# Accumulating DMA transfers for a quarter of the global attention's running sums, and an add on VectorE for the horizontal units

## The chip, the core and the metric

The kernel runs on one core of a Trainium2 chip. Its engines work side by side, each through its own queue of instructions in order: PE (TensorE, matmuls), DVE (VectorE), ACT (ScalarE), POOL (GpSimd) and SP, which here only issues DMA transfers. They wait for one another by semaphores. The metric is the time of one execution on the device in microseconds; several runs are given by their median.

## What is computed

Two layers on eight images of 64 x 64 pixels and 256 channels, all in float32. The first layer has attention in windows of 8 x 64 pixels (horizontal, half of the channels) and 64 x 8 (vertical, the other half), plus a depthwise 3 x 3 convolution, and an output projection. The second has attention of every pixel with all 4096 pixels of its image.

```
# layer 0, cut
s = einsum('bwhtd,bwhsd->bwhts', q, k) / sqrt(d)      # 512 x 512 a window and head, d = 32, 4 heads
a = softmax(s, axis=-1)
ctx = einsum('bwhts,bwhsd->bwhtd', a, v)              # v is k
context = hard_swish(concat(ctx_h, ctx_v) + conv3x3(hard_swish(k)) + bias)
x = context @ w_out + b_out
# layer 1, cut
s = einsum('bnd,bmd->bnm', g, f)                      # 4096 x 4096 an image, d = 32
beta = softmax(s, axis=-1)
v = einsum('bnm,bmd->bnd', beta, h)
out = gamma * (v @ kv + bv) + x
```

The sums of the softmax are what the change is about. The kernel computes exponentials without subtracting a maximum, multiplies them with the values, and divides by their sum afterwards.

## The kernel before

**Units and steps.** An image is cut into units: eight horizontal (`h`), eight vertical (`v`) and two global ones (`l`). A horizontal unit has four steps, a vertical one three, a global one 32. In each step PE computes the scores of 128 keys against four blocks of 512 queries (for a window unit the blocks are the four heads, for a global unit four blocks of pixels), in two PSUM tiles of 128 x 1024. ACT takes the exponential of each (`weights_of`, line 543) and writes a weight tile `p` of 128 partitions (keys) x 4 rows x 512 columns. PE multiplies that with the values into `num` (`weighted`, lines 811, 804 and 1005). The weight tiles come from a pool of three buffers: the exponential of a step can't begin before all readers of the tile three steps earlier are done.

**Sums.** The sum over the keys is a product with a matrix of ones. To spend little of PE on it, VectorE first adds weight tiles into `acc` (128 x 2048), and PE multiplies only the result. In a global unit VectorE adds all 32 tiles (`add`, lines 1014 and 1016: 31 adds), and `sums` (line 1025) makes four products of 512 columns, one for each row, into the four quarters of PE's columns. In a horizontal unit VectorE adds only the tiles of steps 0 and 1 (line 820); `sums` (line 842) then makes three terms: the tile of step 2, that of step 3 in two halves of 256 columns, and `acc` in two halves. ACT copies the sums out of PSUM (line 563), VectorE turns them into reciprocals and multiplies (`norm`). `acc` has one buffer for all units, so a unit's first add waits until the sums before it have been read by PE.

**Order.** The order of all instructions is made by a planner when the kernel is built (`Flow`). Scores and values of the steps form its spine. All else (projections of the next image's input, convolution taps, sums, normalisations, transfers) are tasks in lanes (`pe`, `dve`, `act`, `sp`, `pool` and more) with a due step, needs, and estimated costs (the constants ADD, PROD and so on). Between two steps it fills PE, ACT and VectorE by due time as its own clocks allow. `readers` makes it place the adds that read a weight tile before the exponential that overwrites it. The engines then follow that fixed order. The units run in the order h1 to h7, v0 to v7, h0 of the next image, l0, l1, so that projections and convolution of the next image fill the global stage.

**POOL** writes the zero borders of the convolution's input `hv` (memsets, lines 670 to 675) and copies the rows that two tiles share (lines 678 and 679), and relays a bank from one matmul to another in vertical units. It issues no DMA. The transfers that the kernel has are issued by SP, and at the start by ACT.

`raw` holds the weights of the second layer's three projections until they have been combined with the output projection; `h_sb` holds the turned values `h` of the global attention (written at line 954).

Of the kernel before, what the change touches and what calls it, by code (L numbers as in the profile page):

```python
# [23 lines left out]
D = 32  # L24
NQ = P // D
# [5 lines left out]
def quad(r):  # L31
    return slice(r * D, (r + 1) * D)
# [8 lines left out]
def side(h):  # L41
# [5 lines left out]
DUE = dict(  # L47
    near_k=-4, near_q=0, near_values=-14, clip=-12, swish=-1,
    conv_h0=24, conv_h1=10, conv_h2=10, conv_h3=14, conv_v0=1, conv_v1=8, conv_v2=10, conv_v3=8,
    tap=-10, join_h=13, join_hl=20, join_v=9, context=0, norm=1, release=-8, sums=8, add=-6, adds_h=0, adds_v=0, group_h=0, group_v=1, add2=3, apart=4,  # L50
    fg0=-7, fg2=-2, fg3=20, h0=1, h1=10, values_v=-12, near0=-4, spread0=13, spread1=61,
    conv_first=3, far_swish=1,
)
# [5 lines left out]

SCORES, VALUES, PROD, TURN, DRAIN, PASS, THIRD = 0.96, 0.88, 0.86, 0.65, 0.11, 0.43, 0.5  # L60
EXP, EVICT, COPY, VIEW = 0.97, 0.62, 0.52, 0.42
ADD, NORM, SWISH, TAP, TAPS = 2.36, 2.5, 0.75, 0.75, 1.28
PE_LAG, LAG, SLACK = 0.28, 0.1, 0.3
ISSUE, LOAD, VIA, FETCH, HALO, BEHIND = 0.6, 4.3, 2.6, 2.8, 0.6, 3.0

# [20 lines left out]
class Flow:  # L86
# [5 lines left out]
    def __init__(self):  # L92
        self.t = 0
        self.clock = dict(pe=0.0, act=0.0, dve=0.0, sp=0.0)
        self.lanes = dict(pe=[], turn=[], act=[], dve=[], sp=[], pool=[], res=[])
        self.open = None
        self.held, self.held_more, self.values_due = None, 0.0, False
        self.bank_free = 0.0
        self.half_end = self.exp_end = 0.0
        self.third = False  # L100
        self.apart = 0
# [122 lines left out]
    def step(self, scores, values, passes=2, third=False):  # L224

        c = self.clock
        more = (passes - 2) * PASS
        rest = None  # L230
        self.third = passes > 2
        self.apart += 1
        self.values_due = True
        for task in self.waiting("res"):
            if self.apart >= DUE["apart"] and task.begin() <= c["pe"] + DRAIN or not scores:
                self.apart = 0
                c["pe"] = max(c["pe"] + DRAIN, self.half_end + LAG)
                while not task.done:
                    self.fill_act(c["pe"] + 4 * PROD)
                    self.run(task)  # L240
                    self.fill_dve()
        if scores:
            rest = scores()
            c["pe"] = max(c["pe"], self.banks()) + DRAIN + SCORES + more
            self.third = third
            self.half_end = max(c["act"], c["pe"] - more + PE_LAG) + EXP
            if more:
                self.half_end = max(self.half_end, c["pe"] + PE_LAG) + EXP
            before, self.exp_end = self.exp_end, self.half_end + EXP
            c["act"] = self.exp_end  # L250
        else:
            before = self.exp_end
            c["pe"] = self.half_end = self.exp_end = max(c["pe"], c["act"], c["dve"]) + 3.0
        for task in sorted(self.waiting("turn"), key=lambda k: k.due):
            if self.begin(task) <= c["pe"] + 0.1:
                self.run(task)
        urgent = sorted((k for k in self.lanes["pe"] if k.due <= self.t), key=lambda k: k.due)
        if len(urgent) > 1 and urgent[0] in self.waiting("pe"):
            if self.begin(urgent[0]) <= c["pe"] + 0.1:
                self.require(urgent[0])  # L260
        if self.held:
            self.held()
            c["pe"] = max(c["pe"] + DRAIN, before + LAG) + VALUES + self.held_more
        self.held, self.held_more, self.values_due = values, more, False
        if rest:
            rest()
        self.fill_act(self.late(c["pe"]) - EVICT)
        self.fill_pe()
        self.fill_act(self.late(c["pe"]) + SLACK)
        self.fill_dve()  # L270
        for task in self.waiting("sp"):
            if task.begin() <= self.clock["pe"] + 0.5:
                self.run(task)

        for task in self.waiting("pool"):
            if task.begin() + BEHIND <= self.clock["pe"]:
                self.run(task)
        self.t += 1
# [19 lines left out]
def tile_attention_blocks(  # L298
# [18 lines left out]
    nc = tc.nc  # L317
# [26 lines left out]
    nc.sync.dma_start(out=wqkv_sb, in_=w_qkv.rearrange("(k p) m -> p k m", p=P))  # L344
    bqkv_sb = const.tile([P, 4], F32, name="bqkv_sb")
    nc.sync.dma_start(out=bqkv_sb, in_=b_qkv)
    raw = const.tile([P, 2, 3, D], F32, name="raw")
    for z in range(3):
        nc.scalar.dma_start(out=raw[:, :, z, :], in_=wfgh[z].rearrange("(k p) m -> p k m", p=P))

# [34 lines left out]


    NF = 3 * D + 3
    flat = raw.rearrange("p k z d -> p k (z d)")
    ext = prep.tile([P, 2, NF], F32, name="ext")
    a_f = prep.tile([P, 2, 3], F32, name="a_f")  # L390
    nc.vector.tensor_mul(
# [69 lines left out]
    def attention(images, load_x, out_rows, exact):  # L461
# [9 lines left out]
            tc.tile_pool(name=f"dram{sfx}", bufs=2, space=bass.MemoryType.DRAM)  # L471
        )
        ptp = pools.enter_context(tc.tile_pool(name=f"ptp{sfx}", bufs=3))
        ps_sc = pools.enter_context(tc.tile_pool(name=f"ps_sc{sfx}", bufs=1, space=PSUM))
        ps_av = pools.enter_context(tc.tile_pool(name=f"ps_av{sfx}", bufs=1, space=PSUM))

# [2 lines left out]
        act = [state.tile([P, 2, 2 * TB], F32, name=f"act{i}") for i in range(NB // 2)]  # L479
        f4 = state.tile([P, N], F32, name="f4")  # L480
        gq = state.tile([P, 2, TB], F32, name="gq")
        h_sb = state.tile([P, N // P, D], F32, name="h_sb")


        pairs = deque(ps_sc.tile([P, 2, TB], F32, name=f"s_{i}") for i in range(3))
# [99 lines left out]
        def image(b):  # L585
# [374 lines left out]
            def global_unit(z):  # L960
                nm = f"{b}_l{z}"
                u = {}
# [38 lines left out]
                def weighted(c):  # L1001
                    if c == 0:
                        u["num"] = ps_av.tile([P, TB], F32, tag="num", name=f"num_{nm}")
                    for r in range(NQ):
# [2 lines left out]
                            start=(c == 0), stop=(c == 4 * NB - 1),  # L1007
                        )

                def add(c):  # L1010

                    if c == 1:
                        u["acc"] = work.tile([P, NQ, TB], F32, tag="acc", name=f"acc_{nm}", bufs=1)
                        nc.vector.tensor_add(u["acc"], u[0], u[1])
                    else:
                        nc.vector.tensor_add(u["acc"], u["acc"], u[c])  # L1016
# [5 lines left out]
                def sums():  # L1022
                    u["sum"] = mm_tile(f"sum_{nm}")
                    for r in range(NQ):
                        nc.tensor.matmul(  # L1025
                            u["sum"][quad(r), :], lhsT=ones[:, :D], rhs=u["acc"][:, r, :],
                            start=True, stop=True,
                        )
                    copy_sums(u, nm)

                def norm():
# [40 lines left out]
                def last_ends(m, js):  # L1072
# [12 lines left out]
                        nc.sync.dma_start(out=out_rows(b, m)[:, i * TB : (i + 1) * TB], in_=ot)  # L1085

                return SimpleNamespace(
                    steps=4 * NB, scores=scores, weighted=weighted, add=add,
                    release=release, sums=sums, norm=norm, result=result,
                    last_blocks=last_blocks, last_ends=last_ends,  # L1090
                )
# [57 lines left out]
        for u in units:  # L1149
# [4 lines left out]
            if u.kind == "l":  # L1154
                chain = None
                for c in range(1, u.steps):
                    task = flow.add(
                        "dve", [(partial(u.add, c), [("dve", ADD)])], u.t + c + DUE["add"],
                        [w[c]] + ([w[0]] if c == 1 else [chain]), ready=u.t + c + 1,
                    )  # L1160
                    if c == 1:
                        in_turn("acc", task)
                        readers[u.t].append(task)
                    readers[u.t + c].append(task)
                    chain = task
                total = flow.add(
                    "pe", [(u.sums, [("pe", PROD), ("act", COPY)])], e + 1, [chain], ready=e, bank=True
                )
                in_turn("sum", total)
                last_users["acc"].append(total)  # L1170
# [360 lines left out]
```

## Time and profile before

| | |
|---|---|
| runs | 3416.8, 3414.51, 3416.49 us; median 3416.49 |
| profiled execution, span from first to last instruction | 3412.2 us |
| mean granted TensorE clock | 0.996 |
| adds of global units (line 1016), 128x2048 | 480 of 2.291 us, 1099.7 us in all |
| first adds of global units (line 1014) | 16 of 2.292 us |
| adds of horizontal units (line 820) | 64 of 2.283 us |
| exponentials of global units (line 543), 128x1024 | 1024 of 1.025 us, in 512 pairs |
| one convolution tap on VectorE (line 691) | 1.280 us, 512 of them |
| bytes moved by DMA | 210 MB, mean 62 GB/s |

The span is that of one profiled execution; the runs' times are a little longer, since they hold what lies around the instructions. Busy shares say how much of the span an engine executed something; a matmul's end is modelled, and a PE that waits for a short time can look busy. The columns of the windows view, for each stretch of time, are its length, then busy time and number of instructions of PE, of its weight loads (PEld), DVE, ACT and POOL, then the granted clock, the DMA engines' busy share, and GB/s.

### The profile page before, as it was taken

How to read it: one execution, taken by the hardware profiler on the slowest of the kernel's cores; microseconds unless marked ns; L12 is line 12 of the kernel's file. 1: busy time of each engine (PE TensorE's matmuls, PEld its weight loads, DVE VectorE, ACT ScalarE, POOL GpSimd, SP SyncE). 2: the span in 40 equal slices, each digit the busy share in tenths (PEclk: the TensorE clock that was granted, in tenths of full speed). 3: DMA queues.
4: the chain of work that ended last, by engine and by line, in shares of the span. 5: the costliest groups of instructions: out<-in, count | busy, mean ns of one | idle time of the engine just before them, and what ended most of it. 6: DMA issues, size and time to landing. Idle time of an engine off the chain costs nothing. (4 is left out here: it accounts for less than half of the span.)

```text
span 3412.2 us, 83293 instructions
## 1 busy us (share of the span) xinstructions
PE 3353.6 (98%) x36340; PEld 1260.9 (37%) x36340; DVE 2799.7 (82%) x2340; ACT 2663.0 (78%) x3235; POOL 55.4 (2%) x264
## 2 busy tenths in 40 slices
PE   7999999999999999999999999999999999999998
PEld 3343333533335333353334433344333443334422
DVE  4789798986989779897798887988879888798886
ACT  5778787887778877788778887788877888778776
POOL 0000000000000000000000000000000000000000
PEclk9999999999999999999999999999999999999999
DMA  2132103221033111231112311123111231122201
GB/s 71 51 91 67 50 14 103 85 57 57 19 95 93 49 54 38 88 89 49 44 44 86 93 42 51 51 82 92 42 43 57 86 88 40 38 62 71 73 21 39
DMA packets 249428, 210.13 MB, mean 62 GB/s; under 512 B 26080, under 2 KB 190432, under 8 KB 249056
## 3 DMA queue, kind: packets, MB, share of 16 engines
q1 hardware_dynamic: 246816, 204.18, 20.1%
q8 instruction: 287, 4.70, 0.6%
q10 hardware_dynamic: 2240, 0.56, 0.1%
q14 instruction: 85, 0.70, 0.1%
HBM read 99.78 MB, written 83.89 MB: 54 GB/s over the span
## 5 line engine op out<-in xcount | busy, mean ns | idle before, releaser
L1016 DVE TENSOR_TENSOR acc_l<-acc_l,p_l 128x2048 f32<-128x2048 f32 x480 | 1099.7, 2291 | 229.9 <-ACT p_l L543 204.0
L543 ACT ACTIVATE p_l<-s 128x1024 f32<-128x1024 f32 x1024 | 993.3, 1025 | 202.9 <-PE s L989 136.1
L691 DVE SCALAR_TENSOR_TENSOR act<-hv,dw_sb,act 128x1024 f32<-128x1024 f32 x512 | 654.9, 1280 | 29.5 <-ACT act L687 15.9
L989 PE MATMUL s<-gq,f 32*128 32x512 f32 x4096 | 631.6, 639 | 1.6 <-ACT p_l L543 1.0
L543 ACT ACTIVATE p_h<-s 128x1024 f32<-128x1024 f32 x512 | 494.2, 1023 | 76.7 <-PE s L782 49.3
L1005 PE MATMUL num_l<-p_l,h_sb 128*32 128x512 f32 x4096 | 545.5, 605 | 2.1 <-ACT nums_l L1020 2.1
L294 PE MATMUL pq<-x,wqkv_sb 128*32 128x256 f32 x8192 | 533.2, 383 | 3.0 <-ACT qh L617 1.6
L294 PEld LDWEIGHTS pq<-x,wqkv_sb 128*32 128x32 f32 x8192 | 264.3, 111 | 380.2 <-issue 237.4
L782 PE MATMUL s<-qh,kh 32*128 32x512 f32 x2048 | 316.2, 640 | 9.7 <-ACT qh L617 5.7
L989 PEld LDWEIGHTS s<-gq,f 32*128 32x128 f32 x4096 | 195.0, 182 | 300.4 <-issue 282.7
L811 PE MATMUL num_h<-p_h,vs 128*32 128x512 f32 x2048 | 272.8, 605 | 5.3 <-DMA vs<-kvia 3.5
L759 PE MATMUL s<-qv,kv 32*128 32x256 f32 x3072 | 242.1, 402 | 8.3 <-ACT p_v_m L776 8.3
L294 PE MATMUL s<-act,wout_sb 128*32 128x512 f32 x2048 | 226.7, 594 | 0.1
L1005 PEld LDWEIGHTS num_l<-p_l,h_sb 128*32 128x32 f32 x4096 | 80.6, 108 | 386.1 <-issue 371.3
L804 PE MATMUL num_v<-p_v,vs 128*32 128x256 f32 x2048 | 197.5, 382 | 0.0
L1054 ACT ACTIVATE ot_l<-s,bias_o 128x512 f32<-128x512 f32 x120 | 76.0, 684 | 153.0 <-PE s L294 140.4
L759 PEld LDWEIGHTS s<-qv,kv 32*128 32x128 f32 x3072 | 145.9, 184 | 124.9 <-ACT p_v L771 34.4
L820 DVE TENSOR_TENSOR acc_h<-p_h,p_h 128x2048 f32<-128x2048 f32 x64 | 146.1, 2283 | 18.4 <-PE sum_l L1025 13.2
L771 ACT ACTIVATE p_v<-s 128x1024 f32<-128x1024 f32 x128 | 131.5, 1028 | 35.0 <-PE s L759 35.0
L782 PEld LDWEIGHTS s<-qh,kh 32*128 32x128 f32 x2048 | 92.2, 183 | 174.7 <-issue 136.8
L776 ACT ACTIVATE p_v_m<-s 128x1024 f32<-128x1024 f32 x128 | 131.7, 1029 | 23.1 <-DVE acc_v L827 23.1
L820 DVE TENSOR_TENSOR acc_v<-p_v,p_v 128x2048 f32<-128x2048 f32 x64 | 146.6, 2290 | 0.0
(139 smaller groups left out, 3213.3 us busy)
## 6 DMA issues: line engine op xcount, KB each, us to landing
x<-in_xT SPq DMA_DIRECT2D x92, 512.0 KB, 3.9
kvia<-kt SPq DMA_DIRECT2D x128, 256.0 KB, 2.3
vs<-kvia SPq DMA_DIRECT2D x512, 64.0 KB, 2.0
out<-ot_l SPq DMA_DIRECT2D x128, 256.0 KB, 2.1
via_v<-nums_v SPq DMA_DIRECT2D x64, 256.0 KB, 2.0
shuf_v<-via_v SPq DMA_DIRECT2D x256, 64.0 KB, 2.0
f<-fg SPq DMA_DIRECT2D x256, 64.0 KB, 2.0
gq<-fg SPq DMA_DIRECT2D x64, 64.0 KB, 2.0
```

The costliest lines, as they stand in the source:

```text
L294: nc.tensor.matmul(out[quad(r), :], lhsT=lhsT[:, quad(r)], rhs=rhs, start=start, stop=stop)
L543: nc.scalar.activation(pt[:, 2 * z : 2 * z + 2, :], sc[z], AF.Exp, scale=scale)
L691: nc.vector.scalar_tensor_tensor(o, src, wt, o, ALU.mult, ALU.add)
L759: mm = nc.tensor.matmul(place_of(n, r, h, sc), lhsT=k[quad(r), t * P : (t + 1) * P], rhs=q[quad(r), side(h)], start=True, stop=True,)
L776: nc.scalar.activation(pm, mid, AF.Exp, scale=D**-0.5)
L782: nc.tensor.matmul(row_of(sc, r), lhsT=k[quad(r), c * P : (c + 1) * P], rhs=q[quad(r), :], start=True, stop=not exact,)
L804: nc.tensor.matmul(u["num"][quad(r), side(h)], lhsT=vs[kind, i][:, r, t, :], rhs=place_of(n, r, h, (pt[:, :2], u["mid", c], pt[:, 2:])), s ...
L811: nc.tensor.matmul(u["num"][quad(r), :], lhsT=vs[kind, i][:, r, c, :], rhs=u[c][:, r, :], start=(c == 0), stop=(c == 3),)
L820: nc.vector.tensor_add(u["acc"], u["acc"] if c == 2 else u[0], u[c])
L989: nc.tensor.matmul(row_of(sc, r), lhsT=f4[quad(r), c * P : (c + 1) * P], rhs=gq[quad(r), z, :], start=True, stop=not exact,)
L1005: nc.tensor.matmul(u["num"][quad(r), :], lhsT=h_sb[:, c, :], rhs=u[c][:, r, :], start=(c == 0), stop=(c == 4 * NB - 1),)
L1016: nc.vector.tensor_add(u["acc"], u["acc"], u[c])
```

## The change

Three parts.

1. Global units: VectorE adds only rows 0 to 2 of each weight tile (1536 columns in place of 2048). Row 3 (128x512, 256 KB) is summed by DMA transfers that POOL issues: steps 0 and 1 are copied, the even steps to row 3 of `acc` and the odd steps to a tile `row` of its own, and each later step's transfer adds to what lies there. So there are 32 transfers a unit in two chains, 512 in all. The sums' product for row 3 has two parts, `acc` and `row`, one after the other into the same quarter of PE's columns.
2. Horizontal units: `adds_h=1`, so VectorE adds the third weight tile (step 2) into `acc` as well, with a second add of 128x2048; the sums then have the tile of step 3 as one product of 512 columns, and `acc` in two halves.
3. To have room for `row`, `h_sb` becomes a constant tile, and `raw` a view of its first six blocks.

The planner gets a lane `rows` for the transfers, with estimated costs of 1.0 and 3.0, and a smaller cost for the add.

```diff
-    tap=-10, ... adds_h=0, adds_v=0, ...
+    tap=-10, ... adds_h=1, adds_v=0, ...
...
-ADD, NORM, SWISH, TAP, TAPS = 2.36, 2.5, 0.75, 0.75, 1.28
+ADD, ADD3, NORM, SWISH, TAP, TAPS = 2.36, 1.83, 2.5, 0.75, 0.75, 1.28
+GATHER, SUMMED = 1.0, 3.0
...
+        for task in self.waiting("rows"):
+            if task.begin() <= self.clock["pe"] + 0.5:
+                self.run(task)
         for task in self.waiting("pool"):
...
-    raw = const.tile([P, 2, 3, D], F32, name="raw")
+    h_sb = const.tile([P, N // P, D], F32, name="h_sb")
+    raw = h_sb[:, : 2 * 3, :].rearrange("p (k z) d -> p k z d", k=2)
...
+        rowp = None if exact else pools.enter_context(tc.tile_pool(name="rowp", bufs=1))
...
-        h_sb = state.tile([P, N // P, D], F32, name="h_sb")
...
+                rows = NQ if exact else NQ - 1
+
+                def acc_tile():
+                    if "acc" not in u:
+                        u["acc"] = work.tile([P, NQ, TB], F32, tag="acc", name=f"acc_{nm}", bufs=1)
+                    return u["acc"]
+
                 def add(c):
 
-                    if c == 1:
-                        u["acc"] = work.tile([P, NQ, TB], F32, tag="acc", name=f"acc_{nm}", bufs=1)
-                        nc.vector.tensor_add(u["acc"], u[0], u[1])
+                    acc = acc_tile()[:, :rows, :]
+                    nc.vector.tensor_add(acc, u[0][:, :rows, :] if c == 1 else acc, u[c][:, :rows, :])
+
+                def gather(c):
+
+                    if c < 2:
+                        u["row", c] = (
+                            rowp.tile([P, TB], F32, tag="row", name=f"row_{nm}")
+                            if c else acc_tile()[:, rows, :]
+                        )
+                        nc.gpsimd.dma_start(out=u["row", c], in_=u[c][:, rows, :])
                     else:
-                        nc.vector.tensor_add(u["acc"], u["acc"], u[c])
+                        nc.gpsimd.dma_start(out=u["row", c % 2], in_=u[c][:, rows, :], accum_op=ALU.add)
...
                     for r in range(NQ):
-                        nc.tensor.matmul(
-                            u["sum"][quad(r), :], lhsT=ones[:, :D], rhs=u["acc"][:, r, :],
-                            start=True, stop=True,
-                        )
+                        parts = [u["acc"][:, r, :]] if r < rows else [u["row", 0], u["row", 1]]
+                        for k, part in enumerate(parts):
+                            nc.tensor.matmul(
+                                u["sum"][quad(r), :], lhsT=ones[:, :D], rhs=part,
+                                start=(k == 0), stop=(k == len(parts) - 1),
+                            )
...
-                        "dve", [(partial(u.add, c), [("dve", ADD)])], u.t + c + DUE["add"],
+                        "dve", [(partial(u.add, c), [("dve", ADD if exact else ADD3)])], u.t + c + DUE["add"],
...
+                gathered = []
+                for c in range(0 if exact else u.steps):
+                    task = flow.add(
+                        "rows", [(partial(u.gather, c), [("pool", GATHER), ("dma", SUMMED)])], u.t + c,
+                        [w[c], *gathered[-2:-1]], gathered[-1:], ready=u.t + c + 1,
+                    )
+                    if c < 2:
+                        task.after += last_users["acc"][-1:]
+                    readers[u.t + c].append(task)
+                    gathered.append(task)
                 total = flow.add(
-                    "pe", [(u.sums, [("pe", PROD), ("act", COPY)])], e + 1, [chain], ready=e, bank=True
+                    "pe", [(u.sums, [("pe", PROD * (1 if exact else 1.5)), ("act", COPY)])], e + 1,
+                    [chain, *gathered[-2:]], ready=e, bank=True,
                 )
```

(`exact` marks a second version of the kernel that runs only where sums leave the range of float32; it does not run here.)

More of the change, by code (lines that the diff above doesn't have):

```diff
@@ L49 @@
     conv_h0=24, conv_h1=10, conv_h2=10, conv_h3=14, conv_v0=1, conv_v1=8, conv_v2=10, conv_v3=8,
-    tap=-10, join_h=13, join_hl=20, join_v=9, context=0, norm=1, release=-8, sums=8, add=-6, adds_h=0, adds_v=0, group_h=0, group_v=1, add2=3, apart=4,
+    tap=-10, join_h=13, join_hl=20, join_v=9, context=0, norm=1, release=-8, sums=8, add=-6, adds_h=1, adds_v=0, group_h=0, group_v=1, add2=3, apart=4,
     fg0=-7, fg2=-2, fg3=20, h0=1, h1=10, values_v=-12, near0=-4, spread0=13, spread1=61,
@@ L94, in __init__ @@
         self.clock = dict(pe=0.0, act=0.0, dve=0.0, sp=0.0)
-        self.lanes = dict(pe=[], turn=[], act=[], dve=[], sp=[], pool=[], res=[])
+        self.lanes = dict(pe=[], turn=[], act=[], dve=[], sp=[], pool=[], rows=[], res=[])
         self.open = None
@@ L387, in tile_attention_blocks @@
     NF = 3 * D + 3
-    flat = raw.rearrange("p k z d -> p k (z d)")
+    flat = h_sb[:, : 2 * 3, :].rearrange("p (k z) d -> p k (z d)", k=2)
     ext = prep.tile([P, 2, NF], F32, name="ext")
@@ L1087, in global_unit @@
                 return SimpleNamespace(
-                    steps=4 * NB, scores=scores, weighted=weighted, add=add,
+                    steps=4 * NB, scores=scores, weighted=weighted, add=add, gather=gather,
                     release=release, sums=sums, norm=norm, result=result,
```

## The prediction

> **What bounds the kernel now.** I read the busy shares first, then one image cut into its stages, then who waits for whom, then single steps.
>
> ```profile
> PE 3353.6 (98%) x36340; PEld 1260.9 (37%) x36340; DVE 2799.7 (82%) x2340; ACT 2663.0 (78%) x3235; POOL 55.4 (2%) x264
> ```
>
> The windows view of one image, with its rows in the order horizontal units 1 to 7, vertical units, unit 0 of the next image, the two global units:
>
> ```profile
> 910.00:1023.40 113.40, 112.67 (x1196) 38.84 (x1192) 96.57 (x101) 86.32 (x109) 5.05 (x16) 1.00 0.27 80
> 1023.40:1118.50 95.10, 94.09 (x1273) 48.97 (x1266) 86.96 (x92) 77.96 (x95) 0.78 (x8) 1.00 0.31 93
> 1118.50:1131.70 13.20, 13.20 (x148) 5.08 (x148) 6.38 (x8) 11.11 (x14) 0.00 (x0) 1.00 0.23 66
> 1131.70:1327.60 195.90, 195.63 (x1930) 63.11 (x1932) 158.74 (x89) 156.79 (x189) 1.11 (x8) 1.00 0.13 39
> ```
>
> PE (second number) fills every stage; VectorE (fourth) has 17 us free in the horizontal stage, 8 in the vertical, 37 in the global one. But PE's ends are modelled, so short waits hide in its busy time. The waits view and two stretches of global steps show them:
>
> ```profile
> ACT p_l L543 <- DVE acc_l L1016: 61.7, 106, 2.2
> ```
> ```profile
> 1308.06 1.94 ACT L543 ACTIVATE p_l<-s 128x1024 f32<-128x1024 f32 x2 [0.46 <-DVE acc_l L1016]
> 1310.46 1.94 ACT L543 ACTIVATE p_l<-s 128x1024 f32<-128x1024 f32 x2 [0.46 <-DVE acc_l L1016]
> ```
> ```profile
> 3271.28 1.94 ACT L543 ACTIVATE p_l<-s 128x1024 f32<-128x1024 f32 x2 [0.25 <-PE s L989]
> 3273.43 1.94 ACT L543 ACTIVATE p_l<-s 128x1024 f32<-128x1024 f32 x2 [0.21 <-PE s L989]
> ```
>
> A step without other matmuls takes 2.40 us where the exponential waits for the add that frees its weight buffer (2.29 plus 0.1), and 2.15 us where it waits for PE. So PE bounds the kernel, except in about 106 global steps, where VectorE's add does.
>
> **Third weights of horizontal units: off PE, onto VectorE.**
>
> ```profile
> 942.77 1.07 PE L811 MATMUL num_h<-p_h,vs 128*32 128x512 f32 x8
> 943.65 1.91 PE L842 MATMUL sum_h<-p_h,ones 128*32 128x512 f32 x24
> 945.37 1.05 PE L842 MATMUL sum_h<-acc_h,ones 128*32 128x256 f32 x16
> ```
>
> From 943.65 to 945.37 run 24 matmuls on the weights: 8 of 512 columns (step 2's weights) and 16 of 256 (step 3's, in two halves). Afterwards step 2's are in the accumulated tile and step 3's make one product of 512. 1.72 us for twice the same work is 0.86 each, so PE loses 64 units x 0.86 = 55.0 us. VectorE gains 64 adds of 128x2048 at 2.29 (146.6 us). A global add shrinks to 1536 columns: the adds of 512 columns (L859, 0.692) and 2048 (2.291) give 1.041 ns a column, so 1.758; 496 x 0.533 = 264 us less. VectorE in all: -118 us. Where this lands is read from the instruction order: between the first add of unit 1 and the first vertical add VectorE gets 7 adds (+16.0) and loses 8 convolution taps (8 x 1.28), 4 swishes, 3 joins or contexts and a transpose (8 x 0.69) and one normalisation (2.4), together -18.2. The global stage takes 11 more taps. So the horizontal stage holds 96.6 - 2.2 = 94.4 us of VectorE work in 113.4 - 7 x 0.86 = 107.4: 88% in place of 85%. What hides the new adds is that room; but the sums' last term now follows 0.86 us after the first and waits in PE's queue for the second add, with the next scores behind it. The nearest row is 20.0 us in 15 waits of p_h for acc_h (1.3 each): doubled, +20; at best 0. I take +8, the convolution work having moved away.
>
> **Fifth sum product of a global unit.** The fourth row's sum is made from two parts into one quarter of PE's columns. Four side by side take 0.97 (below, 1227.23 to 1228.20); one more behind the fourth costs up to 0.86, at least 0 if the next matmuls fill the other quarters. I take 0.86: 16 x 0.86 = +13.8.
>
> **The accumulating transfers.** 512 transfers of 128x512 (256 KB), issued on POOL's queue, two chains (even and odd steps), each waiting for the one before it in its chain. The trace has no DMA issued by POOL and none that adds, so their latency L, from the weights being ready to the landing, is bounded by the nearest rows:
>
> ```profile
> x<-in_xT SPq DMA_DIRECT2D x92, 512.0 KB, 3.9
> kvia<-kt SPq DMA_DIRECT2D x128, 256.0 KB, 2.3
> out<-ot_l SPq DMA_DIRECT2D x128, 256.0 KB, 2.1
> ```
>
> From below 2.1 plus 0.33 (SP's median issue): 2.5. From above 3.9, since an addition reads both operands (512 KB as x does), plus 0.87 (SP's longest issue): 4.8. I take 4.3, nearer to the upper end for those 512 KB. That bound holds if adding itself is not slow, which no row here excludes.
>
> [...]
>
> What L costs I find by walking the 512 pairs of global exponentials: each pair keeps its spacing of the trace (2.40 set to 2.15), but may not begin before the transfer three steps earlier has landed (three weight buffers), and a transfer starts at its weights' end or at the landing of the one two steps earlier. At a global unit's change the first two transfers also wait for the old sums on PE, 4.0 and 3.7 us after their own weights. In the changed order the sums stand one step later than here:
>
> ```profile
> 1227.23 1.04 PE L1025 MATMUL sum_l<-acc_l,ones 128*32 128x512 f32 x8
> ```
> ```profile
> 1232.31 1.02 ACT L543 ACTIVATE p_l<-s 128x1024 f32<-128x1024 f32 x1 [0.99 <-PE s L989]
> ```
>
> The sum would begin near 1229.4, its row is read by 1230.3, the first transfer lands 4.3 later at 1234.6, and the exponential of step 3, at 1232.3 before, waits 2.3 for it. Eight times, some 18 us, against about 25 saved in 106 steps x 0.24. The walk gives, in us: L 2.5: -23; 3.5: -15; 4.3: -9; 5.0: +30; 5.5: +76; 6.0: +144; 7.0: +357. Above 5 the chain's pace, L/2 a step, passes the common steps of 2.4 to 2.9.
>
> On POOL's queue the transfers stand among the halo copies and memsets. Two rows:
>
> ```profile
> L678 POOL COPY hv<-hv x48: 231/238/1227, 52.5 to 3074.6; 128x64 f32<-128x64 f32 x48
> ```
> ```profile
> L670 POOL MEMSET hv<- x64: 125/132/136, 16.6 to 3048.7; 128x18 f32 x64
> ```
>
> A copy, which reads, takes up to 1.0 us more than its 0.24 (much as if a convolution tap of 1.28 held it off); a memset, which only writes, never does. [...]
>
> [...]
>
> The other queues: SP's transfers share the 16 DMA engines, 13% busy in the global stage. A transfer of 512 KB lands 1.9 us after one of 64 KB would (3.9 against 2.0), so 256 KB take the engines about 1.1 us and both operands 2.2; 64 of them are 70 to 140 us of 196. Together with the 13% that still fits, and the loads and fetches there are issued steps ahead, so I count 0; if the engines were full, L itself would grow, which rival 1 prices. The last unit's tail: its last transfer lands 4.3 after the last exponential (3383.1), at 3387.4, before the sums at 3389.5: 0.
>
> **Sum.** Span 3412.2 - 55.0 + 13.8 + 8 - 9 = 3370.0. The runs' median, 3416.5, is 4.3 above the span; so 3374 us, -1.2%.
>
> **Rivals.**
> 1. *The transfers become the bound.* Place: the weight buffers of the global steps; price: the walk. It decides from L about 4.9, where the walk eats the 33 that the other terms leave negative (-55 + 13.8 + 8). L 5.5 gives 3460, 6.0 gives 3527, 7.0 gives 3740. For it: nothing in the trace shows an adding transfer, and each must be followed by a landing before the next of its chain. Against: a full 2 x 2.9 us per chain in most steps.
> 2. *VectorE becomes the bound of the horizontal stage.* If each unit's sums wait for the second add for most of its length, 64 x 2.0 = +128 in place of +8: 3494. For it: 85% busy before, and in order. Against: 18.2 us moved out per image.
> 3. *Nothing comes of it*: PE's freed time is taken by later waits, L near 4.9: 3416.
>
> **How the numbers follow.** 0.2% (7 us) is about what a measurement of this kernel can tell from no change. Forecast 0.54, all faster; rival 1 0.26 and rival 2 0.10, slower; rival 3 0.10, of it 0.06 within 0.2% and 0.04 slower. So faster 0.54, same 0.06, slower 0.40. The forecast's own range goes from L 2.5 without the two small costs (-55 - 23: 3338) to L 4.8 (walk +17: 3400). The range for all leaves the lowest end and L above about 5.6 out: 3345 to 3480.
>
> **What would show it.** In the changed profile: PE about 41 us less busy; sum_h on weights 8 matmuls a unit; global adds near 1.76; a POOL transfer landing 3.5 to 4.8 us after its weights; waits of p_l for acc_l nearly gone; few of p_l for a DMA, those at unit changes. The forecast is wrong if p_l waits for transfers in most steps, if global stages grow beyond 196 us, or if sum_h waits long for acc_h.

## The result, and the profile after

The changed kernel takes 3413.93 us (median of 12 runs, 3411.43 to 3416.69); the kernel before, beside it, 3414.39 (12 runs, 3410.46 to 3416.81). The ratio is 1.000, with a 95% interval from 0.9991 to 1.0008: no change that can be measured, where 3374 was forecast. The profiled execution, the longest of the twelve, has a span of 3414.9 us (before 3412.2). Of the runs further below, one of e7 (4641.97 us, at a granted clock of 0.655) is left out.

The busy shares of the kernel after:

```profile
PE 3309.1 (97%) x35348; PEld 1197.4 (35%) x35348; DVE 2662.5 (78%) x2404; ACT 2669.1 (78%) x3235; POOL 518.4 (15%) x776
```

PE is 44.5 us less busy (3353.6 before), which is what the forecast took off it and a little more. But the span has not followed: span less busy time, which is PE's idle time, was 58.6 us and is 105.8. PE lost its work and got 47 us of waiting for it. Behind the first 12 us, PE had 2 waits of over 1 us before, 8.9 us in all; after, it has 22, 44.8 us in all.

The waits of the kernel after (what waited, for what; us in total, times, longest):

```profile
ACT p_v_m L781 <- DVE acc_v L832: 59.5, 61, 3.0
...
ACT p_h L548 <- DVE acc_h L825: 31.3, 26, 1.9
...
PE num_v L809 <- ACT p_v_m L781: 15.4, 9, 2.4
...
ACT p_l L548 <- DMA acc_l<-p_l: 15.0, 9, 2.0
...
ACT p_l L548 <- DVE acc_l L1025: 8.9, 11, 1.2
...
ACT p_l L548 <- DMA row_l<-p_l: 4.7, 7, 1.6
```

The wait that the transfers were to remove is gone: `p_l` for `acc_l` stood at 61.7 us in 106 waits and is 8.9 in 11. `p_l` waits for a transfer 16 times in 512 steps. The new waits are elsewhere: the exponential of a vertical unit's middle part (`p_v_m`) waits for VectorE's add 59.5 us (23.1 before, never over 0.8), and PE waits for that exponential.

A middle image in the windows view, rows as in the prediction: horizontal units 1 to 7, vertical units, unit 0 of the next image, the two global units:

```profile
1764.36:1872.29 107.93, 106.06 (x1044) 33.80 (x1042) 94.04 (x90) 83.67 (x103) 4.30 (x11) 1.00 0.29 83
1872.29:1967.52 95.23, 91.63 (x1220) 44.92 (x1216) 86.26 (x94) 75.63 (x91) 0.33 (x3) 1.00 0.31 87
1967.52:1980.95 13.43, 13.36 (x148) 5.12 (x148) 8.25 (x10) 11.12 (x15) 0.00 (x0) 1.00 0.23 66
1980.95:2179.59 198.64, 198.07 (x2008) 63.87 (x2006) 143.00 (x106) 162.57 (x198) 60.38 (x82) 1.00 0.61 126
```

The horizontal stage lost 5.5 us (113.40 to 107.93), the global one gained 2.7 (195.90 to 198.64). The counts of matmuls (in parentheses after PE's busy time) tell why. The horizontal stage has 152 fewer: the sums of six units stand in it, so the third weights explain 6 x 16 = 96, and 64 are projections (352 to 288; rows cut at the stage's ends make the rest). The vertical stage has 53 fewer, 16 of unit 7's sums and 32 of projections, and is no shorter for it. The global stage has 78 more: 96 of projections and 2 of a fifth sum product, less 16 of unit 0's sums. So 96 matmuls of projections, near 5 us at 0.86 for 16, moved from the first two stages into the global one. The four rows together went from 417.60 us to 415.23.

The same view for the first image, before and then after: horizontal units, then global units.

```profile
23.41:181.27 157.86, 146.48 (x1856) 59.52 (x1852) 102.58 (x107) 114.84 (x153) 5.22 (x23) 0.97 0.20 58
296.12:492.39 196.27, 195.83 (x1928) 63.53 (x1924) 163.01 (x94) 157.33 (x190) 1.11 (x8) 1.00 0.13 38
```
```profile
21.66:186.03 164.37, 139.67 (x1716) 53.96 (x1708) 111.30 (x109) 113.58 (x151) 6.43 (x22) 0.98 0.18 53
304.97:514.53 209.56, 205.91 (x2038) 67.66 (x2030) 155.66 (x118) 164.96 (x202) 60.45 (x82) 0.99 0.59 122
```

With 6.8 us less for PE to do (146.48 to 139.67), the horizontal stage takes 6.5 longer, and the global one, with 110 more matmuls, 13.3 longer. No global stage comes ahead of this image to take its convolution, so VectorE has more to do here than in any other horizontal stage (111.30 us), though that is 68% of its length. Laid side by side, the copies of the sums of global unit 0 out of PSUM come in the eight images later than before by 19.5, 20.7, 19.4, 18.4, 14.5, 14.2, 13.1 and 4.0 us (392.69 against 412.17 in the first, 3299.07 against 3303.09 in the last): the first image loses 20 us that the other seven slowly earn back.

### The profile page after: what moved, and what is told of

Its sections match the earlier page's. It is cut to its first block, busy times and chain, and to the rows that moved or that the text cites. A ratio compares the mean times of both kernels' runs of the same rounds, so it can differ in the third digit from the quotient of the medians.

```text
span 3414.9 us, 82562 instructions
## 1 busy us (share of the span) xinstructions
PE 3309.1 (97%) x35348; PEld 1197.4 (35%) x35348; DVE 2662.5 (78%) x2404; ACT 2669.1 (78%) x3235; POOL 518.4 (15%) x776
## 5 line engine op out<-in xcount | busy, mean ns | idle before, releaser
L1025 DVE TENSOR_TENSOR acc_l<-acc_l,p_l 128x1536 f32<-128x1536 f32 x480 | 843.6, 1758 | 362.6 <-ACT p_l L548 357.8
L994 PE MATMUL s<-gq,f 32*128 32x512 f32 x4096 | 616.2, 640 | 3.6 <-ACT p_l L548 3.4
L787 PE MATMUL s<-qh,kh 32*128 32x512 f32 x2048 | 307.1, 641 | 6.5 <-ACT qh L622 5.7
L1036 POOL DMA_DIRECT2D row_l<-p_l x240 | 219.1, 913 | 549.8 <-ACT p_l L548 493.0
L994 PEld LDWEIGHTS s<-gq,f 32*128 32x128 f32 x4096 | 179.7, 183 | 289.1 <-issue 270.6
L1036 POOL DMA_DIRECT2D acc_l<-p_l x240 | 211.0, 879 | 441.7 <-ACT p_l L548 406.3
L764 PE MATMUL s<-qv,kv 32*128 32x256 f32 x3072 | 228.9, 399 | 4.1 <-ACT p_v L548 2.6
L781 ACT ACTIVATE p_v_m<-s 128x1024 f32<-128x1024 f32 x128 | 131.6, 1028 | 98.8 <-DVE acc_v L832 59.5
L764 PEld LDWEIGHTS s<-qv,kv 32*128 32x128 f32 x3072 | 147.9, 185 | 95.2 <-issue 50.3
```

What stands on the lines that cost most here:

```text
L764: mm = nc.tensor.matmul(place_of(n, r, h, sc), lhsT=k[quad(r), t * P : (t + 1) * P], rhs=q[quad(r), side(h)], start=True, stop=True,)
L787: nc.tensor.matmul(row_of(sc, r), lhsT=k[quad(r), c * P : (c + 1) * P], rhs=q[quad(r), :], start=True, stop=not exact,)
L994: nc.tensor.matmul(row_of(sc, r), lhsT=f4[quad(r), c * P : (c + 1) * P], rhs=gq[quad(r), z, :], start=True, stop=not exact,)
L1025: nc.vector.tensor_add(acc, u[0][:, :rows, :] if c == 1 else acc, u[c][:, :rows, :])
L1036: nc.gpsimd.dma_start(out=u["row", c % 2], in_=u[c][:, rows, :], accum_op=ALU.add)
```

## The experiments

Four theories, as their expectations call them. *Transfer*: the transfers cost more than they bring. *VectorE*: it has no room for the second add (rival 2). *Order*: there is room, but the fixed order now puts a horizontal unit's sums later on PE, and the next unit waits for them. *Buffer*: what such late sums cost is the one `acc` that they keep. No kernel here leaves out part of the computation. "PE idle" is the span less PE's busy time in the one profiled execution of each kernel; the medians are of several runs. The runs were made in batches, and the kernel before beside them went from 3414.39 to 3411.59; counted from it, gains on the changed kernel are 1 to 3 us smaller than the differences of medians given below (e5 25.2, e6 22.4, e8 26.2, e9 10.5, e10 5.0, e11 41.2, e12 51.1).

| kernel | median us | before beside it | ratio, 95% | PE busy | PE idle |
|---|---|---|---|---|---|
| before | 3414.39 | | | 3353.6 | 58.6 |
| after | 3413.93 | 3414.39 | 0.9991 to 1.0008 | 3309.1 | 105.8 |
| e1 adds only | 3513.04 | 3414.07 | 1.0268 to 1.0303 | 3367.5 | 144.0 |
| e2 transfers only | 3414.49 | 3414.07 | 0.9991 to 1.0011 | 3350.5 | 64.1 |
| e3 vertical sums prompt | 3421.18 | 3414.07 | 1.0009 to 1.0029 | 3317.0 | 102.7 |
| e4 all sums prompt | 3405.75 | 3414.07 | 0.9967 to 0.9986 | 3314.6 | 93.9 |
| e5 horizontal sums prompt | 3386.36 | 3411.97 | 0.9913 to 0.9940 | 3293.9 | 86.4 |
| e6 not in the first image | 3389.14 | 3411.97 | 0.9920 to 0.9951 | 3304.4 | 82.4 |
| e7 before, horizontal sums prompt | 3419.30 | 3411.97 | 1.0013 to 1.0032 | 3357.7 | 63.9 |
| e8 = e5 and e6 | 3384.91 | 3411.59 | 0.9911 to 0.9938 | 3307.4 | 79.3 |
| e9 two accumulators | 3400.59 | 3411.59 | 0.9959 to 0.9977 | 3321.2 | 84.4 |
| e10 prompt in the last unit only | 3406.12 | 3411.59 | 0.9973 to 0.9991 | 3305.2 | 99.5 |
| e11 = e8 without unit 1 | 3371.64 | 3413.26 | 0.9862 to 0.9895 | 3303.6 | 65.1 |
| e12 = e11 and two accumulators | 3361.68 | 3413.26 | 0.9835 to 0.9868 | 3295.8 | 63.0 |

### The two halves alone (e1, e2)

e1 is the kernel before with only the second add, e2 the changed kernel without it:

```diff
-    adds_h=0,
+    adds_h=1,
```
```diff
-    adds_h=1,
+    adds_h=0,
```

> The kernel before with only the second half of the change: third weights of horizontal units added on VectorE, global sums as before. PE has 55 us less to do, VectorE 147 us more. Order theory (the sums of the last horizontal unit slide one step back and all vertical units inherit it, so freed PE time turns into waits): 3400 to 3430, with the vertical stage at 95 us or more although PE has 3 us less to do in it. Transfer theory (the transfers and the fifth product took the gain back): about 3416 - 55 + 8 = 3370. VectorE theory (VectorE is full in horizontal and vertical stages, whatever the order): above 3430, since here VectorE gets nothing taken away in the global stage.

> The changed kernel with the third weights of horizontal units back on PE: transfers alone. Order theory: the vertical units' sums stand where they stood before, so the vertical stage keeps its 95 us; global steps gain some 25 us, lose 18 at unit changes and 14 in fifth products: 3405 to 3425. Transfer theory: 3460 to 3475 (the 55 us come back on top of the 3414 measured). VectorE theory: below 3400, since VectorE only loses work (264 us).

Adds alone cost 99 us, in the range of the VectorE theory (above 3430) and outside that of the order theory. The horizontal stage of a middle image in e1 (windows view), and e1's wait for the adds (waits view):

```profile
1367.65:1486.78 119.13, 112.96 (x1132) 37.12 (x1128) 102.33 (x97) 86.28 (x109) 10.51 (x16) 0.99 0.26 81
```
```profile
ACT p_h L543 <- DVE acc_h L820: 70.9, 48, 2.6
```

VectorE's work there grows to 102.33 us, and the stage to 119.13, although PE has less to do; exponentials wait 70.9 us for adds. That reads as if the second add had no room without the transfers, which take some 264 us of adds off VectorE; but it is not shown. The stage is 86% VectorE, and in e1 the order has moved as well: in 39 of 64 horizontal units PE's product of `acc` comes one to three steps after the unit's last values (7 before, 26 in the changed kernel), and 15 first adds begin right at the end of an earlier horizontal unit's sums, behind 71 us of idle time of VectorE. No run gives e1 prompt sums, so the two causes are not separated there. Transfers alone change nothing (+0.4 us; +4.8 forecast). Both halves together leave 3413.93, so on top of the transfers the adds bring -0.6 us where the sum had -47. The transfer theory is out; the question is what became of those 47.

### Where the sums stand (e3, e4, e5, e7)

When a unit's sums become due, the planner still fills PE by due time and can put them behind projections and the next scores. Four kernels force the sums at the next unit's first step that may take them. All have

```diff
         if self.held:
             self.held()
...
+        for task in [k for k in self.lanes["pe"] if k.must == self.t]:
+            self.require(task)
```

and after `total.then = (last, e + DUE["sums"])`, where `e` is that step, one of these: vertical units (e3), all (e4), horizontal units (e5, and e7, where it is put into the kernel before).

```diff
+                if u.kind == "v":
+                    total.must = e
```
```diff
+                if True:
+                    total.must = e
```
```diff
+                if u.kind == "h":
+                    total.must = e
```

> The changed kernel, but a vertical unit's sums are issued in the first step of the unit behind it, as in the kernel before, in place of its second step. Order theory: the vertical stage falls from 95.2-97.1 to 92-93 us, in all 8 images some 20 to 30 us: 3385 to 3397. VectorE theory: nothing, 3410 to 3420, for VectorE is 91% busy there. Transfer theory: nothing, since no transfer runs in the vertical stage.

> The same for horizontal and vertical units alike. Order theory: beside the vertical stages the first image's horizontal stage (164 us, 13 more of PE idle than before) and the others (2 more each) get shorter: 3370 to 3390. VectorE theory: PE now waits for the second add in every horizontal unit, 64 x 1 to 2: 3420 to 3480. Transfer theory: 3410 to 3420.

> The changed kernel, but every horizontal unit's sums are issued in the first step behind the unit, together, in place of being left to the due times; the vertical units are left to them. Order theory (the second add makes the plan put the sums one to three steps later, split around the next scores; they keep the one accumulation buffer, VectorE idles behind it, and the first vertical unit starts late): the first image loses what it gained in length (about -18), each further image some 4 us at the change from horizontal to vertical: 3365 to 3390. VectorE theory (VectorE 87 to 91% busy is the bound whatever the order): PE waits for the second add instead, 3400 to 3430.

> Control: the kernel before with its horizontal sums issued as in the run on the changed kernel. Order theory: its sums stand in the next unit's first or second step already, so nothing: 3408 to 3420. If prompt sums help whatever the kernel, it falls by as much as the changed kernel does.

e3 is a miss: the vertical units, whose exponentials show the largest of the new waits, were not the place; forcing their sums loses 7 us. e4, outside all its ranges, mixes that loss with a gain. e5, horizontal units alone, gains 27.6 us on the changed kernel. The same forcing in the kernel before, where it can move only unit 1's sums of seven images, loses 7.3: it is a remedy for what the second add does to the order, and no gain by itself.

Counted in the same way, no unit of e5 has late sums. First, for comparison, the end of a horizontal stage before, PE and then VectorE:

```profile
1012.86 1.05 PE L842 MATMUL sum_h<-acc_h,ones 128*32 128x256 f32 x16
```
```profile
1017.60 2.25 DVE L820 TENSOR_TENSOR acc_h<-p_h,p_h 128x2048 f32<-128x2048 f32 x1
```

Unit 6's sums end 3.7 us before unit 7's first add, which waits for nothing. The trace of the changed kernel shows the chain, here at the end of a horizontal stage. PE (timeline; start, duration, what; idle time before it in brackets):

```profile
1862.83 1.07 PE L847 MATMUL sum_h<-p_h,ones 128*32 128x512 f32 x8 [0.81 <-ACT qh L622]
1863.83 1.14 PE L787 MATMUL s<-qh,kh 32*128 32x512 f32 x8
1864.90 1.06 PE L816 MATMUL num_h<-p_h,vs 128*32 128x512 f32 x8
1865.78 1.05 PE L847 MATMUL sum_h<-acc_h,ones 128*32 128x256 f32 x16
...
1885.36 0.64 PE L809 MATMUL num_v<-p_v_m,vs 128*32 128x256 f32 x8 [2.38 <-ACT p_v_m L781]
```

VectorE in the same stretch:

```profile
1866.95 2.29 DVE L825 TENSOR_TENSOR acc_h<-p_h,p_h 128x2048 f32<-128x2048 f32 x1 [5.29 <-ACT p_h L548]
...
1870.96 2.29 DVE L825 TENSOR_TENSOR acc_h<-acc_h,p_h 128x2048 f32<-128x2048 f32 x1
...
1880.58 2.28 DVE L825 TENSOR_TENSOR acc_v<-p_v,p_v 128x2048 f32<-128x2048 f32 x1
1882.96 1.23 DVE L832 TENSOR_TENSOR acc_v<-acc_v,p_v_m 128x1024 f32<-128x1024 f32 x1
```

And ACT:

```profile
1884.28 1.02 ACT L781 ACTIVATE p_v_m<-s 128x1024 f32<-128x1024 f32 x1 [3.04 <-DVE acc_v L832]
```

Unit 6's second add had ended at 1859.84, but its sums are split: one term at 1862.83, then a whole step of unit 7, and the term that reads `acc` ends at 1866.83. 0.1 us later VectorE begins unit 7's first add, after 5.29 us of standing idle. (The releaser named is ACT's `p_h`, but the two weight tiles that this add reads were complete at 1861.87; the wait that ended last is the one for PE.) Everything on VectorE behind it is late: unit 7's second add, the normalisation, three taps and, at 1880.58, the first add of vertical unit 0. The exponential that overwrites `p_v_m` waits for it 3.04 us, and PE waits 2.38 for the exponential. This wait of 2.38 us occurs at this place in six images. In all, 10 first adds of the changed kernel begin within 0.2 us of the end of an earlier horizontal unit's sums, behind 47 us of idle time; before, none follows such sums by less than 3.07 us, and in e5 none by less than 3.1. (A first add behind a global unit's sums waits too, 29.5 us in 7 against 13.2 before, but it does so in e11 as well, 24.2 in 6, so that is not the loss.)

e5 puts the sums together and early, and pays for it in another place: in six images PE then waits for the second add itself (e5, timeline of PE).

```profile
1336.73 1.04 PE L850 MATMUL sum_h<-p_h,ones 128*32 128x512 f32 x8
1339.58 1.07 PE L850 MATMUL sum_h<-acc_h,ones 128*32 128x256 f32 x16 [1.81 <-DVE acc_h L828]
```

### The first image, the buffer and the last unit (e6, e8, e9, e10)

e6 leaves the first image's horizontal units as before; e8 joins that to e5:

```diff
-                adds = not exact and DUE["adds_v" if kind else "adds_h"]
+                adds = not exact and DUE["adds_v" if kind else "adds_h"] and b
```

> The changed kernel with the first image's horizontal units as in the kernel before (three sum terms on PE), all others as changed. If the first image's 22 us are its own (there no global stage stands before its horizontal units, so no convolution work can move out of them): 3388 to 3400. If they are handed on to the next image: 3410 to 3420.

> Both remedies: horizontal sums issued at once, and the first image's horizontal units as in the kernel before. Order theory: prompt sums already brought the first image from 493 us to 472, against 470 for its plain units, so hardly more than prompt sums alone: 3378 to 3388. If each remedy pays for itself (27 and 25 us): 3360 to 3368.

e6 comes out 24.8 us below the changed kernel: 8 of the 64 second adds lost as much as the other 56 bring. What happens there is seen on VectorE in the changed kernel (timeline):

```profile
107.28 2.28 DVE L825 TENSOR_TENSOR acc_h<-p_h,p_h 128x2048 f32<-128x2048 f32 x1
109.48 10.60 DVE L696 SCALAR_TENSOR_TENSOR act<-hv,dw_sb,act 128x1024 f32<-128x1024 f32 x8
120.00 2.29 DVE L825 TENSOR_TENSOR acc_h<-acc_h,p_h 128x2048 f32<-128x2048 f32 x1
...
130.45 2.29 DVE L825 TENSOR_TENSOR acc_h<-p_h,p_h 128x2048 f32<-128x2048 f32 x1 [6.36 <-ACT p_h L548]
```

and on PE:

```profile
135.98 1.93 PE L298 MATMUL pq<-x,wqkv_sb 128*32 128x256 f32 x32 [1.86 <-ACT kv L641]
...
149.64 1.06 PE L847 MATMUL sum_h<-p_h,ones 128*32 128x512 f32 x8 [2.17 <-ACT kh L637]
```

Eight convolution taps, 10.60 us, stand between the two adds of one unit; its sums follow only at 129.28 and end at 130.33, and the next unit's first add, at 130.45, has waited 6.36 us for them. After it PE waits for ACT, with projections between. Together with prompt sums (e8) the remedy is worth little more than either: they mend the same loss. The global stage of the first image, which begins at 296.12 us before and at 304.97 in the changed kernel, begins at 294.16 in e6 and at 291.85 in e5: with prompt sums there is room for the second adds in the first image too.

e9 keeps the order's lateness and takes away what it holds: the odd horizontal units accumulate in half of `f4`, a tile that stands free in that stage. e10 forces only the sums of each image's last horizontal unit.

```diff
+                alt = not exact and not kind and i % 2 == 1
...
+                        u["acc"] = f4[:, : NQ * TB].rearrange("p (r c) -> p r c", r=NQ) if alt else work.tile(
...
-                in_turn("acc", acc)
+                in_turn(u.alt, acc)
...
-                last_users["acc"].append(total)
+                last_users[u.alt].append(total)
```
```diff
+                if u.kind == "h" and any(u is im.h[-1] for im in ims):
+                    total.must = e
```

> The changed kernel, but odd horizontal units accumulate in the first half of f4, a tile that is idle in the horizontal stage, so two accumulation buffers alternate; the sums stay as late as in the changed kernel. Buffer theory (the late sums hurt because they keep the one buffer and VectorE idles behind it): most of the 27 us of prompt sums, 3383 to 3400. If late sums hurt by themselves (the normalisation, the joins and convolutions behind them come late; the one product bank is kept): 3405 to 3420.

> The changed kernel with prompt sums for the last horizontal unit of each image alone. It prices the change from horizontal to vertical units: from the stages of the run with all sums prompt, 1 to 2.4 us in each of 7 images: 3397 to 3407, the first image still near 490. If the whole gain sits there: 3383 to 3392. If none: 3410 to 3418.

With two accumulators 13.3 us come back, half of e5's 27.6 and between the two ranges expected. The held `acc` is thus about half of what the late sums cost, roughly: e9's ten runs spread from 3394.30 to 3407.59, the longest at the lowest granted clock (0.993 against 0.996), and it has a wait of its own, PE for `p_h`, 1.13 us in seven images. The last unit alone gives 7.8. The other half is not taken apart further; late sums also make the unit's normalisation and all behind it late, which no run separates.

### What is left, and a faster kernel (e11, e12)

e11 is e8, except that horizontal unit 1 of each image keeps its due times, since forcing it had made PE wait 1.81 us there. e12 adds the two accumulators.

```diff
+                if u.kind == "h" and not any(u is im.h[1] for im in ims):
+                    total.must = e
```

> Both remedies (prompt horizontal sums, first image's units as before), but the second horizontal unit of each image, where PE waited 1.81 us for the second add in six images of the prompt run, is left to the due times. If such PE waits are the loss still open: 3384.9 - 6 x 1.8 = 3374, so 3368 to 3380. If the time only moves to the next wait: 3380 to 3390.

> The same with two accumulation buffers for horizontal units. Buffer theory: with prompt sums VectorE has 3 us or more between the sums' end and the next unit's first add, so a second buffer adds nothing there: within 5 us of the run beside it. If the buffer still binds at the change to the vertical units (there the two-buffer run had 92.8 to 93.1 us where prompt sums had 94.7): 1.7 us less in each of 7 images, 12 in all.

e11 takes 3371.64 us, 42.3 less than the changed kernel; e12 3361.68, which is 1.5% faster than the kernel before (ratio 0.9835 to 0.9868). PE's idle time is back at 65.1 and 63.0. Busy shares of e11, and the four rows of a middle image:

```profile
PE 3303.6 (98%) x35476; PEld 1210.1 (36%) x35476; DVE 2645.7 (79%) x2396; ACT 2665.1 (79%) x3235; POOL 515.8 (15%) x776
```
```profile
1732.77:1837.94 105.17, 104.09 (x1040) 33.34 (x1042) 90.96 (x89) 81.54 (x101) 4.30 (x11) 1.00 0.29 85
1837.94:1932.64 94.70, 93.38 (x1225) 47.14 (x1218) 86.49 (x93) 77.45 (x93) 0.34 (x3) 1.00 0.30 87
1932.64:1945.88 13.24, 13.24 (x148) 5.16 (x148) 11.01 (x12) 11.11 (x15) 0.00 (x0) 1.00 0.26 74
1945.88:2144.94 199.06, 198.33 (x2008) 63.99 (x2006) 143.03 (x106) 162.38 (x198) 60.27 (x82) 1.00 0.61 125
```

The same place as above in e11, PE and then VectorE: unit 6's sums end at 1826.93, unit 7's first add begins 3.9 us later, and the first add of the vertical unit comes at 1844.07, with no wait between PE and `acc`:

```profile
1825.88 1.05 PE L850 MATMUL sum_h<-acc_h,ones 128*32 128x256 f32 x16
```
```profile
1830.82 2.25 DVE L828 TENSOR_TENSOR acc_h<-p_h,p_h 128x2048 f32<-128x2048 f32 x1
...
1833.59 2.29 DVE L828 TENSOR_TENSOR acc_h<-acc_h,p_h 128x2048 f32<-128x2048 f32 x1
...
1844.07 2.29 DVE L828 TENSOR_TENSOR acc_v<-p_v,p_v 128x2048 f32<-128x2048 f32 x1
```

The horizontal stage went from 113.40 us to 105.17. PE's sums on `sum_h` are 5.4 of these 8.2 us (16.79 to 11.43), and its 64 matmuls of projections that moved out are 3.5 (21.45 to 17.95), less 0.9 for a fifth product. The projections come back in the global stage, but the four rows together take 412.17 us where they took 417.60: 5.4 less, and eight products less two fifth products, at 0.86 each, are 5.2. Now the removed work is removed time. e12's further 10 us were expected in the vertical stage and came in the horizontal one (windows view of e12):

```profile
1729.41:1833.29 103.88, 103.20 (x1040) 33.16 (x1042) 91.05 (x89) 81.40 (x100) 3.27 (x11) 1.00 0.29 86
```

The vertical stage stays at 94.7 in both.

## Why the prediction was wrong

**The step that failed** is the price of the sums' wait: "The nearest row is 20.0 us in 15 waits of p_h for acc_h (1.3 each): doubled, +20; at best 0. I take +8". By the runs, the adds on top of the transfers brought -0.6 instead of -47, so this term was about +54, far over its upper end. The prediction had the sums stand right behind their unit and wait in PE's queue for the second add; the waits of the changed kernel have none of PE for `acc_h` there. The row that it doubled prices ACT waiting for VectorE, and did grow much as forecast, by 11.3 us to 31.3 in 26 waits. The cost arose where VectorE waits for PE: in 26 of 64 units the sums came one to three steps late in PE's order, kept the only `acc`, and VectorE stood idle with room to spare, 47 us before 10 first adds. The prediction read VectorE's changed order and counted its instructions stage by stage, and stopped there; it did not read where the horizontal sums themselves had gone, though the text named the single `acc`. The runs show it: with the same instructions in another order 27.6 us return (e5), with the sums no earlier and a second buffer 13.3 (e9), and with prompt sums and the first image's eight second adds taken back 42.3 (e11).

**Third weights off PE**, -55.0, was right in size (for the horizontal stage the prediction counts seven products; six stand in it). PE is 44.5 us less busy, with -55.0 + 13.8 = -41.2 from the two counted terms, and the sums on weights have 8 matmuls a unit. In e11, with 56 of the 64 units changed, 42.9 us against e2 remain of 56 x 0.86 = 48.2. That a stage of 88% VectorE has room was right with the transfers (e11: 90.96 of 105.17). The first image, whose units have many taps between the adds, was not looked at separately; e6 puts what was lost there at 25 us, and e5 shows that it, too, was the order.

**Rival 2**, at 3494, came near the second adds alone (3513.04, e1), but that its cause held there, a full VectorE, is not shown: e1's sums are late as well. Of the 18.2 us that the change moves off VectorE in the horizontal stage, some 10 move out without the transfers too (96.57 + 16.0 for the adds, less the 102.33 of e1). The two halves do not add up: 99 and 0.4 alone, -0.5 together.

**Transfers.** L was forecast at 4.3, bounds 2.5 to 4.8. Measured from the end of the weights to the landing, the median is 3.95 us (the middle 80 in a hundred from 3.68 to 5.89; 110 of 512 took over 4.8, so the upper bound was too low for a fifth of them): issued 0.4 after the weights, landed 3.4 and 3.3 later, as the list of DMA issues of the changed kernel has it (issue, count, KB each, median us from issue to landing):

```profile
acc_l<-p_l POOLq DMA_DIRECT2D x256, 256.0 KB, 3.4
row_l<-p_l POOLq DMA_DIRECT2D x256, 256.0 KB, 3.3
```

Global adds fell to 1.758 us, as computed. The walk had +0.86 and 2.3 at each change from global unit 0 to unit 1; there, in six images, two steps took 3.21 + 2.93 us and take 2.35 + 4.94, +1.15 in all with the fifth product (+0.5 over five steps). Yet the walk's gain of 25 us in common steps is not seen either: transfers alone gave +0.4 for a forecast +4.8, and the reason seems to be that steps which no longer wait for VectorE are filled with projections: the global stage of e2 takes 200.09 us against 195.90, with 2024 matmuls against 1930, and its horizontal stage 110.02 against 113.40, with 1136 against 1196. What shortens one stage lengthens another. **Rival 1** did not occur: 16 waits of `p_l` for transfers, 19.7 us in all. One of the prediction's own signs against itself did, global stages beyond 196 us (198.64), but with projections that moved in.

**POOL's queue** has no term in the sum, and needed none: the issue of an adding transfer takes 0.87 us (0.92 at the most, but for seven of 2.06 to 2.07, each behind halo copies; these take up to 2.95 us now, against 1.26 before, and the memsets up to 0.50, against 0.14). **Other queues** at 0 was near: the DMA engines are 61% busy in the global stage, and the transfers of `x` land 4.1 us after their issue instead of 3.9.

**Rival 3** gave the measured time, 3416, by luck: later waits did take PE's freed time, but its price came from L near 4.9, and L was 3.95.

Open: why the vertical stage, with some 50 fewer matmuls, stays at 94.70 in e11 (in the changed kernel, at 95.23, PE's idle time there is 3.60 us against 1.01, and 2.38 of it is the wait above); how much of e1's loss is order; and the half of the late sums' cost that is not the buffer.

## What to carry to other kernels

When work is taken off the engine that bounds a kernel with a planned order, look up where the order puts the consumers of the shared single buffer afterwards, and price the producer's wait for that buffer, not only the wait for the new producer. Cost each stage that differs (the first image here) by itself. Two edits that use the same engine, one freeing it and one filling it, are priced together: alone each was worth nothing or a loss here.

## What was not expected of the hardware

Short waits of PE can come with a lower granted clock. At the 2.38 us wait behind the end of the horizontal stage, four of six images show one, of 0.50, which begins between 0.7 us before the wait's end and 0.3 after it; two stay at 1.00. A stretch of 8 us with it and one without, and between them the part of the first at the lower clock (windows view of the changed kernel; the granted clock is the third number from the end):

```profile
1466.00:1474.00 8.00, 5.62 (x60) 2.36 (x60) 7.65 (x10) 4.71 (x6) 0.00 (x0) 0.79 0.09 25
1468.12:1471.53 3.41, 2.69 (x20) 0.96 (x20) 3.31 (x6) 2.50 (x3) 0.00 (x0) 0.50 0.00 0
1882.50:1890.50 8.00, 5.62 (x76) 2.56 (x76) 7.65 (x10) 5.27 (x6) 0.00 (x0) 1.00 0.22 62
```

In the first, PE did 60 matmuls in place of 76 in the same busy time. The vertical stage is 96.5 to 97.1 us long in those four images and 95.2 without it, some 6 us in all. The stretches at half clock that begin at 314.42, 635.27, 1468.12, 2300.98 and 2717.40 in this trace each last 3.41 us, and their beginnings lie whole multiples of 3.413 us apart (94, 244, 244 and 122); what sets this is not shown. PE's waits there were 1.87 us at the first, ended 1.2 before, and 2.37 to 2.38 at the others; in e9 half clock came beside waits of 1.13 us (granted clock 0.61 from 2282 to 2286), and in e5 the clock stayed at 1.00 after six of 1.81, so these runs give no length that is safe or not.

An adding transfer of 256 KB between two tiles took 3.3 to 3.4 us to land, where plain ones of that size took 2.1 to 2.5, and 0.87 us of POOL to issue, where its plain copies took 0.57. It thus landed sooner than a plain transfer of 512 KB from `in_xT` (4.1), by which the prediction had bounded it; that the two operands of an addition count as 512 KB was an estimate, and no run shows it.
